# The head of a deformable-convolution stage: inputs asked for first, offsets beside norms, constants beside the sampling

## The chip, the cores and the metric

The kernel runs on one core of a Trainium2 chip. A core has TensorE (PE), VectorE (DVE), ScalarE (ACT), GpSimd (POOL) and SyncE (SP), which run their own instruction streams in order and meet through semaphores, and 16 DMA engines that SP, ACT and POOL give work to. The metric is the device time of one execution in microseconds, as the median of several; lower is better.

## The reference

The model has two layers; only the first half of layer 0 is touched here. For an image `x` of 2 x 128 channels x 64 x 64 pixels:

```python
x = x + L0_conv(ln_c(x))       # layer 0: deformable convolutions, then a small mixture of experts
t = t + L0_ffn(ln_t(t))
x = x + L1_conv(ln_c(x))       # layer 1: a depthwise convolution, a state-space scan, a gated output
t = t + L1_ffn(ln_t(t))        #          then experts that pick their tokens
```

`L0_conv` has four branches of kernel sizes 1, 1, 3 and 7, so 1 + 1 + 9 + 49 = 60 taps. For every pixel and tap, an ordinary convolution of the same size gives an offset in y and x and a mask (180 channels in all); the normalised image is sampled bilinearly at the shifted place, multiplied by the mask, and the samples of all taps are multiplied by the branch's weights and summed:

```python
offset = conv2d(x, off_w, off_b, pad); mask = 2 * sigmoid(conv2d(x, mod_w, mod_b, pad))
sampled = bilinear_sample(x, base_y + off_y, base_x + off_x) * mask     # outside the image: zero
y = einsum('bckhw,ock->bohw', sampled, reg_w)                            # then group norm and relu
```

A fifth branch uses the mean of the image; a 1 x 1 convolution fuses the five.

## The kernel before

**Tiling.** A group is 8 image rows, 512 pixels, handled as four tiles of 128 pixels (`GT`); an image has 8 groups (`NG`), and the batch has two images, `b` = 0 and 1.

**The norm of one group** (`norm_group`, L254 to L287). The input `xc` (128 channels x 512 pixels) is loaded on SP, transposed on PE (L264), copied to `xn` by ACT (L266), and normalised per pixel (`token_norm_gen`, L80: statistics on DVE, square root on ACT, then DVE). Eight DMAs on SP (L280) write `xn` into `table[b]` in DRAM: 67 x 67 places of 4 x 128 values, where a place holds a pixel and its three neighbours, so that one row read is one bilinear sample. `xn` is also transposed back (L271), copied by ACT to `padc`, and written by ACT's queue to `xp[b]`, the padded image (L283); a sum over `padc` (L286) serves the mean. `zero_table` (L236) writes the zero borders first: four rows and four columns of `table[b]`, and the rims of `xp[b]`, on SP.

**The offsets of one group** (`offset_stream`, L297). Rows of `xp` are loaded as `stage` on SP (`rows`, L357); ACT copies them seven times, shifted, into `ring` (`to_ring`, L362); PE does 49 products for each of four pairs of rows (`products`, L369); DVE adds the bias, and after each second pair `corners` (L388) works out indices and weights for half of the group.

**The sampling of one group** (`sample`, L535) goes through the 60 taps: four indirect gathers on POOL (L547) into one of six `v` buffers, bilinear weighting on DVE, transposes and summing on PE, a copy to `st` on ACT, and, two taps later, the product with the tap's weights `regw` (L597). The weights come in six chunks of ten taps; `load_chunk` (L231) loads one into one of four places.

**What sets the order.** There is no scheduler in this part: each engine runs its instructions in the order in which the program issues them. Python generators cut the side work into steps: `together` and `mixed` (L157) step several norms in turn, and `sample` takes after each tap one step of `conv` (the offsets of the next groups) and two or three steps of `rest` (three for the first group). `rest` holds the norm of image 1, then `more` (a second PSUM place for the offsets), then `position_matrices` (L845), which prepares layer 1. `self.pending` holds functions that `sample` calls after a counted number of taps.

**The head.** The program's first DMAs are three constants in `Env` (L61 to L66) and those of layer 1's `L1Conv.__init__` (L885 to L910). Then `run` (L457) opens the pools, writes the zero borders of image 0, normalises its eight groups three at a time, loads weights on ACT's queue (`load_weights`, L218) and four chunks on SP, writes the zero borders of image 1, works out the offsets of group 0, and starts to sample.

Of the kernel before, what the change touches and what calls it, by code (L numbers as in the profile page):

```python
# [3 lines left out]

# [51 lines left out]
class Env:  # L56
    def __init__(self, tc, ctx, d):
        self.tc, self.nc, self.d = tc, tc.nc, d
        cp = ctx.enter_context(tc.tile_pool(name="const", bufs=1))
        nc = self.nc  # L60
        self.ident = cp.tile([P, P], F32, name="ident")  # L61
        nc.sync.dma_start(out=self.ident, in_=d["c_ident"])
        self.gm16 = cp.tile([P, P], F32, name="gm16")
        nc.sync.dma_start(out=self.gm16, in_=d["c_gm16"])
        self.gm8 = cp.tile([P, P], F32, name="gm8")
        nc.sync.dma_start(out=self.gm8, in_=d["c_gm8"])  # L66
        self.zero = cp.tile([P, 512], F32, name="zero")
        nc.vector.memset(self.zero, 0.0)

# [107 lines left out]
class L0Conv:  # L177
# [40 lines left out]
    def load_weights(self):  # L218
        nc, d = self.env.nc, self.env.d
        nc.scalar.dma_start(out=self.wcen, in_=d["wcen"])  # L220
        nc.scalar.dma_start(out=self.wring, in_=d["wring"])
        nc.scalar.dma_start(out=self.wout, in_=d["wout"])
        nc.scalar.dma_start(out=self.obias, in_=d["obias"].partition_broadcast(P))
        nc.scalar.dma_start(out=self.base, in_=d["c_base"])
        nc.scalar.dma_start(out=self.gn, in_=d["gn"])
        nc.scalar.dma_start(out=self.gnf, in_=d["gnf"])
        for c in range(3):
            self.load_chunk(c)
        self.load_chunk(5)

    def load_chunk(self, c):  # L231

# [3 lines left out]
    def zero_table(self, b):  # L236
        nc, z = self.env.nc, self.env.zero
        t = self.table[b]
        rows = t.rearrange("(y x) e -> y x e", x=TW)
        for y in (0, 1, TW - 2, TW - 1):  # L240
            nc.sync.dma_start(out=rows[y], in_=z[:TW, :512])
        for x in (0, 1, TW - 2, TW - 1):
            nc.sync.dma_start(out=rows[2 : TW - 2, x, :], in_=z[: TW - 4, :])
        for y in (0, 3 + H):
            nc.sync.dma_start(
                out=self.xp[b][:, y : y + 3, :], in_=z[:, : 3 * (W + 6)].rearrange("p (y x) -> p y x", y=3)
            )

    def norm(self, b, pp, tag):
        for g in range(NG):  # L250
            yield from self.norm_group(b, g, self.sp, pp, tag)
        yield from self.norm_end(b)

    def norm_group(self, b, g, sp, pp, tag):  # L254


        env, nc = self.env, self.env.nc
        tab = self.table[b].rearrange("(y x) e -> y x e", x=TW)
        xp = self.xp[b]
        xc = sp.tile([P, 512], F32, name="xc")  # L260
        nc.sync.dma_start(out=xc, in_=env.d["x"][b, :, g * 512 : (g + 1) * 512])
        yield
        pt = pp.tile([P, GT, P], F32, name="nrm_pt", tag=tag)
        transpose4(nc, env.ident, pt, [xc[:, j * P : (j + 1) * P] for j in range(GT)])  # L264
        xn = sp.tile([P, GT, C], F32, name="xn")
        nc.scalar.copy(xn, pt)  # L266
        yield
        yield
        yield from token_norm_gen(env, sp, "n0", xn, xn, 1e-6)
        pb = pp.tile([P, GT, P], F32, name="pad_pt", tag=tag)  # L270
        transpose4(nc, env.ident, pb, [xn[:, j, :] for j in range(GT)])  # L271
        at = self.padc[g % 2][:, :, 3 : 3 + W]
        nc.scalar.copy(at, pb.rearrange("p j (y x) -> p (j y) x", x=W))
        for dy in range(2):
            for dx in range(2):
                q = 2 * dy + dx
                to = tab[2 - dy : 2 - dy + H, 2 - dx : 2 - dx + W, q * C : (q + 1) * C]
                to = to.rearrange("(t two) x c -> two x t c", two=2)
                for yl in range(2):
                    nc.sync.dma_start(  # L280
                        out=to[yl][:, g * GT : (g + 1) * GT, :], in_=xn[yl * W : (yl + 1) * W, :, :]
                    )
# [11 lines left out]
        self.normed.add(b)  # L294
        yield

    def offset_stream(self, runs):  # L297

        nc = self.env.nc
        chain = iter(())
        todo = deque()

        def piece():

            nonlocal chain
            if todo:
                wait, what = todo[0]
                if wait:  # L310
# [1 line left out]
                else:  # L312
# [1 line left out]
                    k, po, raw, end = what  # L314
                    nc.vector.tensor_tensor(raw[:, k % OT, :], po, self.obias, ALU.add)
                    if end:
                        yield from chain
                        chain = end()
            next(chain, None)
            yield  # L320

        for b, g, dst in runs:
            assert b in self.normed
            idx, w4 = dst or self.new_group(self.op)
            yb = 8 * g
            stage = self.rows(b, yb, 8)
            yield from piece()
            self.to_ring(stage, 0, 8)
            yield from piece()
            for k in range(GT):  # L330
                mats = self.products(2 * k)
                for i in range(7):
                    for m in mats[7 * i : 7 * i + 7]:
                        m()  # L334
# [14 lines left out]
                todo.append((5 if len(self.p_f) > 1 else 0, (k, self.po, raw, end)))  # L349
                if len(self.p_f) == 1:  # L350
                    yield from piece()
        while todo:
            yield from piece()
        for _ in chain:
            yield

    def rows(self, b, y0, n):  # L357
# [99 lines left out]
    def run(self, build, after):  # L457
# [3 lines left out]
        with ExitStack() as ctx:  # L461
# [24 lines left out]
            psum = ctx.enter_context(ExitStack())  # L486
            self.p_f = deque([pools(psum)("l0po", 1, space=PSUM)])
            early = psum.enter_context(ExitStack())
            p_m = pools(early)("l0pm", 1, space=PSUM)

            def more():

                early.close()
                self.p_f.append(pools(psum)("l0po2", 1, space=PSUM))
# [40 lines left out]
    def sample(self, b, g, idx, w4, conv, rest, pace):  # L535

        env, nc = self.env, self.env.nc
        pw = None
        for br, (k, _) in enumerate(BRANCH):
            for t in range(FIRST[br], FIRST[br] + k * k):  # L540
                tw = t % HT
                if tw == 0:
                    pw = self.p_w.tile([P, GT, HT, 4], F32, name="pw")
                    nc.vector.tensor_copy(pw, w4[:, :, t : t + HT, :])
                v = self.vp.tile([P, GT, 4 * C], F32, name="v")
                for j in range(GT):
                    nc.gpsimd.indirect_dma_start(  # L547
                        out=v[:, j, :],
                        out_offset=None,
                        in_=self.table[b],  # L550
                        in_offset=bass.IndirectOffsetOnAxis(ap=idx[:, j, t : t + 1], axis=0),
                    )
                v4 = v.rearrange("p j (q c) -> p j q c", q=4)


# [313 lines left out]
class L1Conv:  # L869
# [4 lines left out]
    def __init__(self, env, dp, wp, x2, x3):  # L874
        nc, d = env.nc, env.d
        self.env, self.dp, self.x2, self.x3 = env, dp, x2, x3
        self.pos = dp.tile([512 // CG, KP, NPOS, CG], F32, name="pos")

        def load(name, shape, src=None):
# [4 lines left out]
        self.wp = wp  # L884
# [19 lines left out]
        self.w1 = [wp.tile([P, 2, 4], F32, name=f"w1_{b}") for b in range(B)]  # L904
        for b in range(B):
            for h in range(2):
                nc.sync.dma_start(out=self.xsd[b][h * P : (h + 1) * P, 0:3], in_=env.zero[:, 0:3])
            for s in range(2):
                nc.sync.dma_start(out=self.att[b][s : s + 1, 0:3], in_=env.zero[0:1, 0:3])
                nc.sync.dma_start(out=self.att[b][s : s + 1, N + 3 :], in_=env.zero[0:1, 0:3])  # L910

    def convs(self, b, sp, pp):

# [694 lines left out]
def metaformer_kernel(ctx: ExitStack, tc: tile.TileContext, d: dict, out: bass.AP):  # L1608
# [7 lines left out]
    with tc.manual_schedule(engines={ET.PE, ET.DVE, ET.Activation, ET.Pool, ET.SP}), ExitStack() as l0:  # L1616
# [102 lines left out]
```

## Time and profile before

| | us |
|---|---|
| median of 3 runs | 8280.49 (8272.83 to 8282.75) |
| the profiled execution | 8332.4 |
| its span | 8330.6 |
| first table write of image 0 issued on SP | 45.19 |
| last table write of image 0 begun | 120.6 |
| first product of the offsets on PE | 164.35 |
| first gather on POOL | 197.88 |
| first gather of group 0's second half | 224.77 |

| engine | busy us | share | instructions |
|---|---|---|---|
| PE | 5808.5 | 70% | 27808 |
| DVE | 5729.7 | 69% | 8508 |
| ACT | 2120.9 | 25% | 4432 |
| POOL | 4590.5 | 55% | 4576 |

The span runs from the first to the last instruction of the profiled execution. In a line of the timeline, the first number is the start in us from the start of the span, the second is the duration in us, then come the engine (SPq and ACTq are DMA issues on those engines' queues), the line of the program, the operation, the tiles written and read, and how many instructions are merged; in brackets stands how long the engine had been idle and what ended that. In a line of the waits: who waited for whom, us in total, times, the longest.

### The profile page before, as it was taken

How to read it: one execution, taken by the hardware profiler on the slowest of the kernel's cores; microseconds unless marked ns; L12 is line 12 of the kernel's file. 1: busy time of each engine (PE TensorE's matmuls, PEld its weight loads, DVE VectorE, ACT ScalarE, POOL GpSimd, SP SyncE). 2: the span in 40 equal slices, each digit the busy share in tenths (PEclk: the TensorE clock that was granted, in tenths of full speed). 3: DMA queues.
4: the chain of work that ended last, by engine and by line, in shares of the span. 5: the costliest groups of instructions: out<-in, count | busy, mean ns of one | idle time of the engine just before them, and what ended most of it. 6: DMA issues, size and time to landing. Idle time of an engine off the chain costs nothing. (4 is left out here: it accounts for less than half of the span.)

```text
span 8330.6 us, 83751 instructions
## 1 busy us (share of the span) xinstructions
PE 5808.5 (70%) x27808; PEld 4000.1 (48%) x27808; DVE 5729.7 (69%) x8508; ACT 2120.9 (25%) x4432; POOL 4590.5 (55%) x4576
## 2 busy tenths in 40 slices
PE   2688888888888867766766676666755565855558
PEld 2456656666666644443434443344434444733335
DVE  1577777777777776777786667666647745669981
ACT  1111111111111113211111221112163344655540
POOL 0456666666666666666666666666534433347640
PEclk7788999999999988888888888788876665656568
DMA  4677666666666668867677777777653344434434
GB/s 128 185 249 216 195 207 203 205 213 197 207 203 206 208 212 261 270 213 234 218 240 203 228 204 223 219 206 216 176 166 135 127 110 107 128 106 149 145 124 141
DMA packets 636007, 1579.35 MB, mean 190 GB/s; under 512 B 167700, under 2 KB 247356, under 8 KB 623036
## 3 DMA queue, kind: packets, MB, share of 16 engines
q0 software_dynamic: 307200, 1006.88, 40.6%
q1 hardware_dynamic: 298284, 515.10, 19.5%
q10 hardware_dynamic: 30096, 52.03, 1.7%
q8 instruction: 226, 3.70, 0.2%
q14 instruction: 201, 1.65, 0.1%
HBM read 1456.11 MB, written 120.01 MB: 189 GB/s over the span
## 5 line engine op out<-in xcount | busy, mean ns | idle before, releaser
L547 POOL DMA_INDIRECT v<-table,idx x3840 | 3643.7, 949 | 2384.2 <-issue 1000.0
L597 PE MATMUL out<-st,regw 128*128 128x512 f32 x3840 | 2115.3, 676 | 161.2 <-issue 108.7
L558 DVE TENSOR_TENSOR v<-v,pw 128x1024 f32<-128x1024 f32 x960 | 1169.5, 1218 | 1060.9 <-DMA v<-table,idx 871.0
L568 PE MATMUL pst<-ident,v 128*128 128x128 f32 x7680 | 1240.2, 304 | 823.3 <-issue 529.5
L577 ACT COPY st<-pst 128x512 f32<-128x512 f32 x960 | 558.3, 585 | 4347.3 <-remote 2367.5
L568 PEld LDWEIGHTS pst<-ident,v 128*128 128x128 f32 x7680 | 1001.1, 157 | 1162.1 <-issue 786.9
L564 DVE TENSOR_TENSOR v<-v,low 128x512 f32<-128x512 f32 x1920 | 1318.0, 686 | 65.4
L563 DVE TENSOR_TENSOR low<-v,pw 128x512 f32<-128x512 f32 x1920 | 1329.0, 692 | 33.4
L1246 POOL TENSOR_TENSOR db<-du,bcb 128x512 f32<-128x512 f32 x512 | 660.0, 1293 | 937.2 <-DVE da L1303 897.4
L597 PEld LDWEIGHTS out<-st,regw 128*128 128x128 f32 x3840 | 762.0, 221 | 776.6 <-issue 713.7
L334 PEld LDWEIGHTS po<-wout,ring 128*128 128x128 f32 x5120 | 740.1, 198 | 366.5 <-issue 365.1
L334 PE MATMUL po<-wout,ring 128*128 128x147 f32 x5120 | 785.6, 299 | 167.4 <-issue 162.3
L1303 DVE TENSOR_TENSOR_SCAN da<-da,state,db 128x512 f32<-128x512 f32 x512 | 657.1, 1283 | 278.3 <-ACT da L1253 260.8
L1271 PE MATMUL py<-ident,sc 128*128 128x128 f32 x2048 | 463.0, 379 | 336.2 <-DVE sc L1313 335.1
L1271 PEld LDWEIGHTS py<-ident,sc 128*128 128x128 f32 x2048 | 338.6, 196 | 476.8 <-DVE sc L1313 441.5
L1313 DVE TENSOR_TENSOR sc<-da,bcb 128x512 f32<-128x512 f32 x512 | 354.2, 692 | 48.6 <-DVE da L1303 1.9
L1253 ACT ACTIVATE da<-delta,w_A_log 128x512 f32<-128x512 f32 x512 | 354.0, 692 | 17.3 <-DVE delta L1209 1.5
L972 PE MATMUL ps<-tm,X 120*88 120x48 f32 x2048 | 246.1, 299 | 62.9 <-ACT Y L924 22.5
L972 PEld LDWEIGHTS ps<-tm,X 120*88 120x88 f32 x2048 | 241.7, 213 | 94.4 <-issue 41.4
L959 PE MATMUL ps<-ident,hs 64*120 64x64 f32 x1408 | 142.1, 271 | 124.9 <-ACT X L924 69.8
L988 PE MATMUL ps<-ident,Y 88*64 88x88 f32 x768 | 108.1, 291 | 155.9 <-ACT img L924 100.1
L959 PEld LDWEIGHTS ps<-ident,hs 64*120 64x120 f32 x1408 | 125.5, 177 | 184.2 <-ACT X L924 89.5
(270 smaller groups left out, 4811.1 us busy)
## 6 DMA issues: line engine op xcount, KB each, us to landing
bcb<-bc SPq DMA_DIRECT2D x256, 512.0 KB
regw<-in_regw SPq DMA_DIRECT2D x66, 1280.0 KB
v<-table,idx POOLq DMA_INDIRECT x3840
yd<-ys ACTq DMA_DIRECT2D x128, 256.0 KB
yc<-yd SPq DMA_DIRECT2D x32, 1024.0 KB
gb<-gd SPq DMA_DIRECT2D x16, 2048.0 KB
wt<-in_weight SPq DMA_DIRECT2D x32, 1024.0 KB
tm<-pos SPq DMA_DIRECT2D x16, 1440.0 KB
```

The costliest lines, as they stand in the source:

```text
L334: m()
L547: nc.gpsimd.indirect_dma_start(out=v[:, j, :], out_offset=None, in_=self.table[b], in_offset=bass.IndirectOffsetOnAxis(ap=idx[:, j, t : t ...
L558: nc.vector.tensor_tensor(up, up, w, ALU.mult)
L563: nc.vector.tensor_tensor(low, v4[:, two, 2:4, :], w, ALU.mult)
L564: nc.vector.tensor_tensor(up[:, two], up[:, two], low, ALU.add)
L568: nc.tensor.matmul(pt[:, j, :], v4[:, j, q, :], env.ident, is_transpose=True, start=j == 0 and q == 0, stop=j == GT - 1 and q == 1,)
L577: nc.scalar.copy(st, pt.rearrange("p j t -> p (j t)"))
L597: nc.tensor.matmul(self.out[half], self.regw[t // CH][:, t % CH, half * P : (half + 1) * P], st, start=first, stop=last,)
L972: nc.tensor.matmul(ps[:, c, :], X[:, c0 + c, :], tm[:, :, c0 + c], start=True, stop=True)
L1246: nc.gpsimd.tensor_tensor(dbs[u], pieces[k]["du"][:, half, :], bcb[u // 2][:, 0, :], ALU.mult)
L1271: nc.tensor.matmul(out[:, j, :], what[:, j * P : (j + 1) * P], env.ident, is_transpose=True, start=first and j == 0, stop=last and j == GT ...
L1303: nc.vector.tensor_tensor_scan(s, s, dbs.pop(u), state[:, half, n : n + 1], ALU.mult, ALU.add)
```

## The change

There are five edits.

1. Constants. Two of the three in `Env` go to ACT's queue. Those of layer 1 move from `L1Conv.__init__` into a generator, `constants`, which `run` puts into the side stream ahead of `position_matrices`.
2. Input. All eight `xc` of image 0 are loaded at once, into two of the `v` buffers, which the sampling doesn't use yet; `load_weights` follows on ACT's queue, and it loads no chunks any more.
3. Norms and offsets. Two norms of image 0 are done, then the 14 rows that group 0 needs are loaded as one `stage0`. The other six go on three at a time: 24 steps first, then one piece of the offsets for every three steps. `offset_stream` takes the loaded rows as `ahead`. When the norms are through, chunk 0 is loaded and the offsets are finished.
4. Side stream. The zero borders of image 1 become steps of `norm`; chunks 1, 2 and 5 go into `pending`, after 1, 10 and 30 taps.
5. Gathers. For the first five taps of group 0, the gathers of the first half of the pixels are issued ahead, and those of the second half at each tap.

```diff
 class Env:
-        nc.sync.dma_start(out=self.gm16, in_=d["c_gm16"])
+        nc.scalar.dma_start(out=self.gm16, in_=d["c_gm16"])
...
-        nc.sync.dma_start(out=self.gm8, in_=d["c_gm8"])
+        nc.scalar.dma_start(out=self.gm8, in_=d["c_gm8"])
...
     def load_weights(self):
...
-        for c in range(3):
-            self.load_chunk(c)
-        self.load_chunk(5)
...
     def zero_table(self, b):
...
         for y in (0, 1, TW - 2, TW - 1):
             nc.sync.dma_start(out=rows[y], in_=z[:TW, :512])
+            yield
         for x in (0, 1, TW - 2, TW - 1):
             nc.sync.dma_start(out=rows[2 : TW - 2, x, :], in_=z[: TW - 4, :])
+            yield
...
     def norm(self, b, pp, tag):
+        yield from self.zero_table(b)
         for g in range(NG):
             yield from self.norm_group(b, g, self.sp, pp, tag)
...
-    def norm_group(self, b, g, sp, pp, tag):
+    def norm_group(self, b, g, sp, pp, tag, xc=None):
...
-        xc = sp.tile([P, 512], F32, name="xc")
-        nc.sync.dma_start(out=xc, in_=env.d["x"][b, :, g * 512 : (g + 1) * 512])
-        yield
+        if xc is None:
+            xc = sp.tile([P, 512], F32, name="xc")
+            nc.sync.dma_start(out=xc, in_=env.d["x"][b, :, g * 512 : (g + 1) * 512])
+            yield
...
-    def offset_stream(self, runs):
+    def offset_stream(self, runs, ahead=None):
...
-            stage = self.rows(b, yb, 8)
+            stage = ahead or self.rows(b, yb, 8)
...
-                        stage = self.rows(b, yb + 2 * k + 8, 2)
+                        stage = ahead[:, 2 * k + 8 :] if ahead else self.rows(b, yb + 2 * k + 8, 2)
...
     def run(self, build, after):
...
-            self.zero_table(0)
+            psum = ctx.enter_context(ExitStack())
+            right = lambda name: pools(psum)(name, 1, space=PSUM, side="right")
+            self.p_f = deque([right("l0po")])
+            cur = self.new_group(self.ip)
...
-                together([self.norm_group(0, g, sp, pp, "nrm") for g in range(NG)], 3)
-            self.load_weights()
-            self.zero_table(1)
-            for _ in self.norm_end(0):
-                pass
+                xs = []
+                for g in range(NG):
+                    if g % GT == 0:
+                        x = self.vp.tile([P, GT, 4 * C], F32, name="v")
+                    xs.append(x[:, g % GT, :])
+                    nc.sync.dma_start(out=xs[g], in_=env.d["x"][0, :, g * 512 : (g + 1) * 512])
+                self.load_weights()
+                for _ in self.zero_table(0):
+                    pass
+                norms = [self.norm_group(0, g, sp, pp, "nrm", x) for g, x in enumerate(xs)]
+                together(norms[:2], 2)
+
+                stage = sp.tile([P, 14, W + 6], F32, name="stage0", bufs=1)
+                nc.sync.dma_start(out=stage, in_=self.xp[0][:, 0:14, :])
+                others = Side()
+                others.add(mixed(norms[2:], 3))
+                for _ in range(24):
+                    others.step()
+                offsets = self.offset_stream([(0, 0, cur)], stage)
+                while others.todo:
+                    next(offsets)
+                    for _ in range(3):
+                        others.step()
+                self.load_chunk(0)
+                for _ in self.norm_end(0):
+                    pass
+                for _ in offsets:
+                    pass
...
+            self.pending = [(n, functools.partial(self.load_chunk, c)) for n, c in ((1, 1), (10, 2), (30, 5))]
...
-            cur = self.new_group(self.ip)
-            for _ in self.offset_stream([(0, 0, cur)]):
-                pass
...
     def sample(self, b, g, idx, w4, conv, rest, pace):
...
+        def gather(v, t, tiles):
+            for j in tiles:
+                nc.gpsimd.indirect_dma_start(
+                    out=v[:, j, :],
+                    out_offset=None,
+                    in_=self.table[b],
+                    in_offset=bass.IndirectOffsetOnAxis(ap=idx[:, j, t : t + 1], axis=0),
+                )
...
+                if b == 0 and g == 0 and t == 0:
+                    for i in range(5):
+                        vs[i] = self.vp.tile([P, GT, 4 * C], F32, name="v")
+                        gather(vs[i], i, range(0, 2))
+                if t in vs:
+                    v = vs.pop(t)
+                    gather(v, t, range(2, GT))
+                else:
+                    v = self.vp.tile([P, GT, 4 * C], F32, name="v")
+                    gather(v, t, range(GT))
...
 class L1Conv:
...
+    def constants(self):
+        nc, d, wp = self.env.nc, self.env.d, self.wp
...
         self.saw = load("sa_conv_w", [14, 1])
+        yield
...
                 nc.sync.dma_start(out=self.att[b][s : s + 1, N + 3 :], in_=self.env.zero[0:1, 0:3])
+            yield
...
-        conv.run(position_matrices(env, mixer.pos), after)
+        conv.run(chain(mixer.constants(), position_matrices(env, mixer.pos)), after)
```

More of the change, by code (lines that the diff above doesn't have):

```diff
@@ L3 @@
 from contextlib import ExitStack
+from itertools import chain
 import concourse.bass as bass
@@ L295, in norm_end @@
         yield
-    def offset_stream(self, runs):
+    def offset_stream(self, runs, ahead=None):
         nc = self.env.nc
-        chain = iter(())
+        arith = iter(())
         todo = deque()
         def piece():
-            nonlocal chain
+            nonlocal arith
             if todo:
@@ L316, in piece @@
                     if end:
-                        yield from chain
-                        chain = end()
-            next(chain, None)
+                        yield from arith
+                        arith = end()
+            next(arith, None)
             yield
         for b, g, dst in runs:
-            assert b in self.normed
+            assert ahead or b in self.normed
             idx, w4 = dst or self.new_group(self.op)
             yb = 8 * g
-            stage = self.rows(b, yb, 8)
+            stage = ahead or self.rows(b, yb, 8)
             yield from piece()
@@ L351, in offset_stream @@
                     yield from piece()
+            ahead = None
         while todo:
             yield from piece()
-        for _ in chain:
+        for _ in arith:
             yield
@@ L485, in run @@
             self.p_o = pool("l0py", 2, space=PSUM)
-            psum = ctx.enter_context(ExitStack())
-            self.p_f = deque([pools(psum)("l0po", 1, space=PSUM)])
+            self.pending = [(n, functools.partial(self.load_chunk, c)) for n, c in ((1, 1), (10, 2), (30, 5))]
             early = psum.enter_context(ExitStack())
-            p_m = pools(early)("l0pm", 1, space=PSUM)
+            p_m = pools(early)("l0pm", 1, space=PSUM, side="right")
             def more():
                 early.close()
-                self.p_f.append(pools(psum)("l0po2", 1, space=PSUM))
+                self.p_f.append(right("l0po2"))
                 yield
-            cur = self.new_group(self.ip)
-            for _ in self.offset_stream([(0, 0, cur)]):
-                pass
             conv, rest = Side(), Side()
@@ L537, in sample @@
         env, nc = self.env, self.env.nc
-        pw = None
+        pw, vs = None, {}
+        def gather(v, t, tiles):
[6 more added lines that the diff above has]
+                )
         for br, (k, _) in enumerate(BRANCH):
@@ L544, in sample @@
                     nc.vector.tensor_copy(pw, w4[:, :, t : t + HT, :])
[L545 to L552, printed above, removed]
+                if b == 0 and g == 0 and t == 0:
[8 more added lines that the diff above has]
+                    gather(v, t, range(GT))
                 v4 = v.rearrange("p j (q c) -> p j q c", q=4)
@@ L877, in __init__ @@
         self.pos = dp.tile([512 // CG, KP, NPOS, CG], F32, name="pos")
+        self.wp = wp
+    def constants(self):
+        nc, d, wp = self.env.nc, self.env.d, self.wp
         def load(name, shape, src=None):
@@ L882, in load @@
             return t
-        self.wp = wp
         self.c1w = load("conv1d_w", [P, 2, 4])
@@ L906, in __init__ @@
             for h in range(2):
-                nc.sync.dma_start(out=self.xsd[b][h * P : (h + 1) * P, 0:3], in_=env.zero[:, 0:3])
+                nc.sync.dma_start(out=self.xsd[b][h * P : (h + 1) * P, 0:3], in_=self.env.zero[:, 0:3])
             for s in range(2):
-                nc.sync.dma_start(out=self.att[b][s : s + 1, 0:3], in_=env.zero[0:1, 0:3])
-                nc.sync.dma_start(out=self.att[b][s : s + 1, N + 3 :], in_=env.zero[0:1, 0:3])
+                nc.sync.dma_start(out=self.att[b][s : s + 1, 0:3], in_=self.env.zero[0:1, 0:3])
+                nc.sync.dma_start(out=self.att[b][s : s + 1, N + 3 :], in_=self.env.zero[0:1, 0:3])
+            yield
     def convs(self, b, sp, pp):
```

## The prediction

> **What bounds the kernel now.** I read the page's slices first: POOL, which gathers for the sampling, shows nothing before the second slice and then 4 to 6 tenths for three quarters of the span. Sampling is the long stage, and nothing of it runs in the first 200 us. The list of waits over the first 500 us says how long:
>
> ```profile
> POOL v L547 <- DMA stage<-xp: 197.4, 1, 197.4
> POOL v L547 <- DVE idx L431: 24.5, 1, 24.5
> ```
>
> So a head of 224.77 us (the gather that the second line ends with) stands before the first complete tap. SyncE's queue over that head, in order of time:
>
> ```profile
> 20.92 7.46 SPq L243 DMA_DIRECT2D table<-zero  x4
> 28.43 1.22 SPq L245 DMA_DIRECT2D xp<-zero  x2
> 29.70 5.99 SPq L261 DMA_DIRECT2D xc<-in_x  x3
> 45.19 17.88 SPq L280 DMA_DIRECT2D table<-xn  x24
> 63.17 1.50 SPq L261 DMA_DIRECT2D xc<-in_x  x3
> 73.22 18.16 SPq L280 DMA_DIRECT2D table<-xn  x24
> 91.48 1.03 SPq L261 DMA_DIRECT2D xc<-in_x  x2
> 101.68 19.51 SPq L280 DMA_DIRECT2D table<-xn  x16
> 121.24 5.17 SPq L234 DMA_DIRECT2D regw<-in_regw  x4
> 129.56 15.23 SPq L241 DMA_DIRECT2D table<-zero  x4
> 144.83 5.33 SPq L243 DMA_DIRECT2D table<-zero  x4
> 150.20 3.35 SPq L245 DMA_DIRECT2D xp<-zero  x2
> 153.60 41.78 SPq L359 DMA_DIRECT2D stage<-xp  x5
> ```
>
> One queue strings everything together: zeros of table 0, norms in threes whose input is asked for only behind the previous three's writes, weights, zeros of table 1, and only then the rows for the offsets. The timeline gives the rest of the head, the four products of 49 matmuls each, whose first one waits for the ring's copies and whose last one ends with the bias addition:
>
> ```profile
> 162.10 3.76 ACT L365 COPY ring<-stage 128x512 f32<-128x512 f32 x7 [58.03 <-DMA stage<-xp]
> ...
> 164.35 0.97 PE L334 MATMUL po<-wcen,ring 128*128 128x180 f32 x2 [60.91 <-ACT ring L365]
> ...
> 219.59 0.35 DVE L315 TENSOR_TENSOR raw<-po,obias 128x180 f32<-128x180 f32 x1 [12.62 <-PE po L334]
> ```
>
> Behind the head I looked at stretches, for the tile st alone; the fourth pair of figures is ACT's copies of it, one per tap (then clock, DMA share, GB/s):
>
> ```profile
> 332.00:384.00 52.00, 16.76 (x26) 6.31 (x25) 0.00 (x0) 3.51 (x6) 0.80 0.71 219
> ...
> 2000.00:2500.00 500.00, 183.97 (x340) 64.11 (x338) 0.00 (x0) 49.63 (x85) 0.91 0.68 204
> ```
>
> Six taps take 52 us while image 1 is normalised; later 85 take 500, 5.88 us each. No later stage waits for a fixed moment, so what the head loses the end loses.
>
> [...] from 15 to 25 us the DMA share is 0.07 at 25 to 26 GB/s, about one sixteenth. [...]
>
> **The change, part by part.**
>
> *Removed from the front.* 8.5 us of constants on SP (2.12 to 10.64); two gm loads go to ACT. All eight x loads go out at about 1.2 us, so the input no longer waits behind table writes.
>
> *The zeros become the first limit.* Table writes overlap the zeroed border, so they wait for it. [...] first table write near 43.5. The first two norms are ready by then: ACT was held 12.7 us after wout before (107.97 to 120.67); shared with x and zeros I allow it until 23, and the first norm took 5.6 us from copy to table write (39.58 to 45.19).
>
> *Norms 0 to 4.* 16 table writes at 17.88/24 = 0.745 us end at 55.4. With three xn buffers, norm 4's copy waits for norm 1's writes; landing is about 3 us (the last xc load issued near 92.0 to PE at 94.85): 58.4. From the last copy of a trio to its first write took 2.75 us (42.44 to 45.19): 61.2. 24 writes: 79.1; landed 82.1. The stage load of 14 rows sits between and is ready.
>
> *Where the offsets start.* Only 24 steps are taken ahead, exactly norms 2, 3, 4. But then the first round issues the ACT copies of norms 5, 6, 7 before the ring copies. The third needs norm 4's buffer, so at 82.1 it goes, at 82.7 the ring copies begin, and PE starts 2.25 later (162.10 to 164.35): 85.0. The offsets thus run beside the tail of three norms, not beside six.
>
> *From there to sampling.* Before: 164.35 to 224.77 = 60.4 us. Added on PE: 12 transposes of norms 5 to 7, 2.45 + 1.2 = 3.6 us. Their normalising takes DVE until about 8 us after the third copy; PE's first 28 matmuls last as long (28/49 of 13.5), so no further wait. The last 24 writes leave SP by about 107; the first half's gathers come near 122. Second half: 85.0 + 60.4 + 3.6 = 149. Against 224.77: **-76 us**.
>
> *Zeros of table 1, chunks.* They have no producer to wait for; SP runs ahead to them right after chunk 0, around 110, [...] ended by 145, hidden by products 1 to 3 and the corners. If that cover were gone, up to 26 us would come back at the first taps. Chunks 1, 2 and 5 are issued at taps 1, 10, 30 for products at 12, 22, 52; ten taps at 5.88 are 59 us: nothing. That SP no longer does this ahead of the offsets (121.24 to 153.60) is in the 76 already.
>
> *Half gathers of five taps.* Eight more gathers at 1.25 us go before the second half's indices. Tap 0 starts as before; for taps 1 to 4 POOL needs 2.5 us rather than 5.0, while DVE needs 4: at most 4 us, I take **-2**.
>
> *The first group's taps.* Norm 1 now starts 8 steps later, at three steps a tap, so its pieces fall otherwise. Before, the sum over padc stands in the tap of its own transposes, and DVE idles 6.65 us for it (at 325.47), and 2.4 us more at statistics and normalising; after, the sum falls a tap later, but the statistics come in the tap of their own transposes and wait for the same queue on PE, some 6.5 us. Net up to -2.5 us in each of 8 cycles of 26 us; as the trace doesn't show that order, bounds +20 and -20, I take **-8**. Also taps 2 to 3 stood 26 us apart (247.16 to 273.48), 15 more than in a later cycle, when table writes met gathers and two stores; three plain taps now go ahead. Bounds 0 and -15: **-5**.
>
> *Constants in the side stream.* 21 small DMAs on SP, hidden, as SP idles between norms. The exponential on ACT waits at worst for its load and has a 1.28 us table load and a reload: 0 to +5, I take **+2**. The gm loads on ACT: 0.9 us before the weights, hidden by the zeros; uncovered +1.
>
> Sum: -76 - 2 - 8 - 5 + 2 = -89 us. The profiled execution took 8332.4 with a span of 8330.6, so 8243 for it; the median of the three runs is 8280.5, 52 lower, and a stretch of the head should be equally long in both: **8191 us**, 1.1% less. A change under 0.2% (17 us) couldn't be told from none.
>
> **Rivals.** *Fuller overlap, 17%.* [...] PE starts at 72 and the first group gives its whole -39: 76 + 13 + 39 - 2 = 126, so about 8155. For it: DMA reached 448 GB/s (110 to 115 us) with large rows. [...]
>
> *The first group takes part back, 18%.* SP gets to table 1's zeros late [...]: +26, and the new order of norm 1 costs +20 instead of -8: -76 + 26 + 20 + 2 - 2 = -30 at the worst; half of both is about 8227. For it: SP's waits [...] (7.14 us for one row under load). Against: SP has 40 us in hand.
>
> *Slower, 2%.* The statistics' wait in the new order of norm 1 comes on top of the old wait for the sum and holds DVE, PE and gathers in turn. It decides where 76 + 17 us are lost, 11.6 us in each of eight cycles, from 26 to 38 us; with 13 us a cycle it is 8280.5 - 76 + 104 = 8308. Against: the longest idle now is 6.65, and one more of that size in each cycle gives 53 in all, 8257.
>
> *No change, 2%:* ACT can't free itself from weight issue (12.7 us became 70), and norms start late.
>
> **How the numbers follow.** Likeliest, 61%: -65 to -112, so 8168 to 8216. Eight in ten, with most of the two side cases: 8156 to 8230. Faster 0.95 (61 + 17 + most of 18, less a point), same 0.03, slower 0.02.
>
> **What would show it.** First table write near 43; PE's first product near 85, directly after ring copies that follow the last xn copy; the 11th gather (second half's indices) near 149; table 1's zeros on SP between 105 and 145; cycles of norm 1 near 24 us. Wrong if: PE starts products before 72 or after 100, the 3-tap cycle leaves 20 to 29 us, or later taps leave 5.88 us.

## The result, and the profile after

| | before | after |
|---|---|---|
| median (range), us | 8278.98 (8272.83 to 8282.75, 4 runs) | 8167.34 (8160.73 to 8177.89, 4 runs) |
| ratio, 95% interval | | 0.9867 [0.985, 0.9884] |
| profiled execution's span | 8330.6 | 8176.1 |
| first table write of image 0 | 45.19 | 48.98 |
| last table write of image 0 begun | 120.6 | 100.3 |
| first product of the offsets | 164.35 | 79.01 |
| first gather of group 0's second half | 224.77 | 145.26 |
| first store of image 1's indices (about 76 taps in, early in the second group) | 744.0 | 652.9 |

The kernel became 112 us faster (interval 96 to 124); 89 were forecast, just outside this interval. In the list of waits over the first 500 us, POOL's wait of 197.4 us for `stage` is gone. What stands ahead of the sampling now are two waits for indices, for the first half and then for the second:

```profile
POOL v L567 <- DVE idx L434: 132.4, 2, 113.1
```

SyncE's queue in order of time, as it was shown of the kernel before:

```profile
1.18 6.79 SPq L488 DMA_DIRECT2D v<-in_x  x8
9.66 16.73 SPq L239 DMA_DIRECT2D table<-zero  x4
26.44 7.49 SPq L242 DMA_DIRECT2D table<-zero  x4
33.98 6.96 SPq L245 DMA_DIRECT2D xp<-zero  x2
48.98 11.72 SPq L282 DMA_DIRECT2D table<-xn  x16
60.74 0.61 SPq L496 DMA_DIRECT2D stage<-xp  x1
61.46 40.42 SPq L282 DMA_DIRECT2D table<-xn  x48
101.92 0.60 SPq L232 DMA_DIRECT2D regw<-in_regw  x1
...
103.05 8.38 SPq L239 DMA_DIRECT2D table<-zero  x3
...
134.70 0.99 SPq L263 DMA_DIRECT2D xc<-in_x  x1
```

The two pauses for input between table writes are gone, and the zeros of table 1 come after the table writes, while PE works. What still stands in front is the zeros of table 0: 31 us of issuing (9.66 to 40.94), and 8 more until the first write. The timeline of ACT and PE shows what the offsets waited for:

```profile
23.89 0.33 ACTq L224 DMA_DIRECT2D obias<-in_obias  x1
34.91 0.33 ACTq L225 DMA_DIRECT2D base<-in_c_base  x1
41.16 0.34 ACTq L226 DMA_DIRECT2D gn<-in_gn  x1
...
42.09 1.28 ACT L268 ACT_TABLE_LOAD   x1 [42.09 <-DMA xp<-zero]
...
76.28 0.58 ACT L268 COPY xn<-nrm_pt 128x512 f32<-128x512 f32 x1 [5.15 <-DMA table<-xn]
76.77 3.76 ACT L368 COPY ring<-stage 128x512 f32<-128x512 f32 x7
...
81.70 0.59 ACT L268 COPY xn<-nrm_pt 128x512 f32<-128x512 f32 x1 [1.07 <-DMA table<-xn]
```

```profile
79.01 0.97 PE L336 MATMUL po<-wcen,ring 128*128 128x180 f32 x2 [7.97 <-ACT ring L368]
...
125.35 0.57 PE L336 MATMUL po<-wcen,ring 128*128 128x180 f32 x2 [3.61 <-issue]
```

ACT's small weight loads are strung out until 41.7 us, although each takes 0.33 us to issue, so ACT's first copy comes only when SP has issued its last zeros (40.94). The ring's copies follow the second of the last three norms' copies, not the third. And the fourth product starts 3.6 us after PE was ready for it.

The 79.5 us of the head divide at instants of these profiles (with those of the run with the offsets behind the norms, below): the end of SP's table-write issue moved from 121.2 to 98.9 with input asked for first (-22.3, of which the run with input asked for late, below, gives back 16); the products' start against that end from +43.1 to -7.9, as weights, chunks and the zeros of table 1 no longer stand between (-51.0); offsets begun beside norms -12.0; and from first product to second half 66.3 instead of 60.4 us (+5.8). The split is read from instants: no run puts weights, chunks and the zeros of table 1 back in front, so the -51.0 rests on what the two queues show. The sum closes by construction, as the third run's instants cancel in it; they lie within 3 us of the changed kernel's where both have the same work.

### The profile page after: what moved, and what is told of

It reads as the page before. It is cut to its first block, busy times and chain, and to the rows that moved or that the text cites. A ratio compares the mean times of both kernels' runs of the same rounds, so it can differ in the third digit from the quotient of the medians.

```text
span 8176.1 us, 83726 instructions
## 1 busy us (share of the span) xinstructions
PE 5782.7 (71%) x27808; PEld 4002.8 (49%) x27808; DVE 5727.6 (70%) x8508; ACT 2122.1 (26%) x4433; POOL 4589.2 (56%) x4576
## 5 line engine op out<-in xcount | busy, mean ns | idle before, releaser
L635 PE MATMUL out<-st,regw 128*128 128x512 f32 x3840 | 2073.0, 665 | 117.9 <-issue 86.5
L336 PE MATMUL po<-wout,ring 128*128 128x147 f32 x5120 | 806.0, 301 | 216.3 <-issue 212.4
```

Of the source, the lines that this page charges most:

```text
L635: nc.tensor.matmul(self.out[half], self.regw[t // CH][:, t % CH, half * P : (half + 1) * P], st, start=first, stop=last,)
```

## Experiments

The runs below come in three sets, each on another chip, and the core's speed in the sampling differs between them: the kernel before took 8343, 8294 and 7557 us, with clocks of 0.80 to 0.84, while the instants of the head stay the same within 3 us up to the start of the products. Only kernels of one set are compared in us; across sets, by their ratio to the kernel before. A set's intervals are some 0.2% either way (17 us), so small effects are read from instants in the profiles. Behind the start of the products, instants differ between sets too.

### Is the excess over the forecast real?

Both kernels were run once more, unedited (first set).

> The changed kernel once more, unedited, for a second profile and more times. The measured gain of 112 us is 23 more than the forecast sum. Theory A (the excess is real and lies in the sampling of image 0): the groups of image 0 are stored at 323 to 325 us intervals again, against 327.4 in the kernel before, and the median is 8155 to 8180. Theory B (the excess is the spread of single executions): the interval moves by 2 us or more between the two profiles of the same kernel.

> The kernel before, unedited, for a second profile of it. Theory A: intervals between the stores of image 0's groups of 327 to 328 us again, and the head to the first gather of the second half 224 to 226 us. Theory B: intervals between 324 and 327 us, and the whole span nearer to the median (8275 to 8285) than the first profile's 8330.6.

The changed kernel took 8233.78 us, the one before 8342.56; ratio 0.9871 [0.9852, 0.989], -109 us. In microseconds from the span's start:

| | before | before again | after | after again |
|---|---|---|---|---|
| second half's first gather | 224.8 | 227.3 | 145.3 | 150.6 |
| first tap of the second group begun | 652.0 | 654.5 | 558.0 | 561.3 |
| first store of image 1's indices | 744.0 | 748.5 | 652.9 | 654.7 |
| eighth store | 3035.8 | 3044.4 | 2923.5 | 2945.9 |
| mean interval of stores (the last is half as long) | 327.4 | 328.0 | 324.4 | 327.3 |
| last group of image 1 done (fuse weights asked for) | 6073.9 | 6073.6 | 5928.3 | 5987.8 |
| span | 8330.6 | 8336.9 | 8176.1 | 8249.9 |

The changed kernel's own interval moved by 2.9 us, which is theory B's outcome; the kernel before kept its interval (328.0), which is theory A's. What decides is the set. From the first store to the end, the four profiles of the first set take 7585 to 7595 us, whichever kernel it is; the four of the second set take 7532 to 7546, one of them the kernel before with wide zeros, and all four have a mean interval of 324.2 to 324.6. The first pair of profiles falls on both sides: 7587 before, 7523 after. The profiled execution before, 8332.4 us, also lies outside the runs beside which it stands (8272.83 to 8282.75) and inside those of the first set (8323.15 to 8351.73). So the 63 us by which the first pair of spans differs beyond the first store (-154.5 against -91.1) come, as far as the record tells, from two sets that were compared with each other, not from the change; the second pair, of one set, shows 7 us less at the end than at the first store (-87.0 against -93.8).

The head and the first group are worth -94 and -93 (at the second group's first tap), and no later gain appears within a set. The medians are 16 to 18 us further down, with -94 and -93 at the edge of their intervals (-96 and -92 us); whether some of that is real stays open.

### Zero rows in 128 pieces

```diff
         for y in (0, 1, TW - 2, TW - 1):
-            nc.sync.dma_start(out=rows[y], in_=z[:TW, :512])
+            flat = t[y * TW : (y + 1) * TW, :].rearrange("x e -> (x e)").rearrange("(p f) -> p f", p=P)
+            nc.sync.dma_start(out=flat, in_=z[:, : TW * 4 * C // P])
...
         for x in (0, 1, TW - 2, TW - 1):
-            nc.sync.dma_start(out=rows[2 : TW - 2, x, :], in_=z[: TW - 4, :])
+            nc.sync.dma_start(out=rows[1 : TW - 2, x, :], in_=z[: TW - 3, :])
```

In the changed kernel:

> The changed kernel with the zero borders written [...] rows as 128 pieces of 1072 bytes, columns of 64 pixels. Theory 1 (the zero rows [...] set the first table write and hold ACT's weight issues until 42 us): ACT is free by 18 to 25 us, the first table write comes at 25 to 32 us instead of 49, the first gather of the second half at 122 to 130 instead of 145.3, and the time falls by 15 to 22 us. Theory 2 (ACT is held by its own large weight load, and SP's zeros only fill that time): ACT is free at 38 to 42 us as now, and the time moves by less than 5 us.

The edit widens the columns too (63 places become 64), so rows and columns aren't told apart. 8215.8 us, ratio 0.9848 [0.9826, 0.9869], 18 us under the changed kernel of the same set. ACT and SP of this run:

```profile
20.97 0.34 ACTq L224 DMA_DIRECT2D obias<-in_obias  x1
...
25.45 1.28 ACT L269 ACT_TABLE_LOAD   x1 [25.45 <-DMA table<-zero]
```

```profile
9.52 7.88 SPq L240 DMA_DIRECT2D table<-zero  x4
21.01 2.44 SPq L243 DMA_DIRECT2D table<-zero  x4
...
32.35 11.96 SPq L283 DMA_DIRECT2D table<-xn  x16
```

ACT comes free 16.6 us earlier, the first table write 16.6, the first product 16.5 (62.46). Theory 1 holds: nothing was changed on ACT's queue, so SP's transfers held ACT's weight loads, and the zeros set the start of everything. The second half's first gather, 133.5, is 3.5 us later than expected, for the late addition seen below.

The same edit in the kernel before (second set):

> The kernel before with the zero borders written [...] nothing else changed. Theory 1 (each set of zeros costs the kernel before [...] some 23 us, of which 14 to 16 are uncovered): the first norms' input arrives at 20 to 25 us instead of 38, the first product begins 26 to 34 us earlier than 164 to 167, and the time falls by 25 to 33 us. Theory 2 (SP's issue of so many transfers is what costs): less than 10 us.

The 23 us of theory 1 was an estimate; 4 x 134 KB of rows at the 25 to 26 GB/s that the kernel before shows from 15 to 25 us make some 21. The run took 8257.15 us, ratio 0.9957 [0.9941, 0.9973]: -37 us by the medians of the set, -22 to -49 by the interval. Its timeline:

```profile
20.71 2.79 PE L104 MATMUL nrm_pt<-ident,xc 128*128 128x128 f32 x12 [20.71 <-DMA xc<-in_x]
```

Input arrives at 20.7 instead of 38.4, the first product begins at 132.8 instead of 164.4, the second half at 192.9 instead of 224.8. So 32 of the old head's 225 us were two sets of zero borders in their narrow form. The change covered the second set, and kept the first.

### Offsets after the norms

```diff
-                while others.todo:
-                    next(offsets)
-                    for _ in range(3):
-                        others.step()
+                others.drain()
```

> The changed kernel with all eight norms finished before the first piece of the offsets; everything else stays. Theory 1 (the offsets only run beside the tail of the last norms, most of the gain is the freed SP queue): PE starts the products at 92 to 97 us instead of 79, the second half's first gather comes at 154 to 160 us, and 9 to 14 us are lost. Theory 2 (running beside the norms hides the products): 40 to 55 us are lost.

8255.27 us, ratio 0.9899 [0.988, 0.9919], 21 us over the changed kernel of the set, with spans only 4 apart (8254.1 and 8249.9). In its timeline:

```profile
91.03 0.97 PE L336 MATMUL po<-wcen,ring 128*128 128x180 f32 x2 [3.93 <-ACT ring L368]
```

12 us later than in the changed kernel (78.9); the second half comes at 159.3, 9 to 14 later. Products that start so soon leave no room for theory 2. "Beside six norms" is worth some 12 us of the head, not the 54 of the products; the loss in time is 4 to 21, and not known more closely.

### Input asked for late

Each input is loaded, into the same `v` buffers, at its norm's first step (third set):

```diff
-                    nc.sync.dma_start(out=xs[g], in_=env.d["x"][0, :, g * 512 : (g + 1) * 512])
...
+        else:
+            nc.sync.dma_start(out=xc, in_=env.d["x"][b, :, g * 512 : (g + 1) * 512])
```

> The changed kernel with each group's input asked for at that norm's first step, as in the kernel before (into the same buffers), instead of all at the start; the order of all else stays. Theory 1 (the input standing behind table writes on SP was a large part of the old head): the first table write comes within 4 us of 49, but norms 2 to 4 start their writes 8 to 12 us later than 61, norms 5 to 7 again so, PE starts the products at 96 to 106 us instead of 79, and 18 to 28 us are lost. Theory 2 (table writes, which take 0.75 us each whatever is done, set the pace anyway): less than 8 us are lost.

7468.11 us against 7556.59 of the kernel before; ratio 0.9885 [0.9862, 0.9908]. SP's queue has the pauses again:

```profile
45.21 11.69 SPq L284 DMA_DIRECT2D table<-xn  x16
56.94 0.61 SPq L497 DMA_DIRECT2D stage<-xp  x1
57.59 1.39 SPq L266 DMA_DIRECT2D v<-in_x  x3
68.50 1.92 SPq L284 DMA_DIRECT2D table<-xn  x3
```

Norms 2 to 4 write 7 us later, norms 5 to 7 at 97.9, the products start at 94.7, 16 later, and so does the second half: 156.4, against 140.2 in the run of the changed kernel (without the early gathers, below) whose last bias additions are as regular as this one's. Theory 1's direction is right, its size a little high at the products. By ratio to the kernel before (0.9867 to 0.9871 for the changed kernel) the loss in time is inside the intervals; but the next run, of the same set, is 16.5 us faster, and the ranges don't overlap (7466.33 to 7476.77, 7441.92 to 7459.59). If the place of the constants is worth nothing in time, the late input thus costs there about what it costs at the products.

### Constants in front

The generator `constants` is run through at the end of `L1Conv.__init__`, and leaves the side stream.

```diff
         self.wp = wp
+        for _ in self.constants():
+            pass
...
-        conv.run(chain(mixer.constants(), position_matrices(env, mixer.pos)), after)
+        conv.run(position_matrices(env, mixer.pos), after)
```

> The changed kernel with layer 1's constants loaded at the start again, before the input. Theory 1 (SP's queue is the path from its first instruction on): the input and the zeros go out 8.5 us later, the first table write comes at 56 to 58 us, the second half's first gather 7 to 9 us later, and 6 to 9 us are lost. Theory 2 (ACT's weight issues, held to 42 us, cover it): the first table write moves by less than 3 us and nothing measurable is lost.

7451.65 us, ratio 0.9856 [0.9832, 0.988]. The first table write came at 50.97 and the first product at 80.9, each 2 us later than in the changed kernel; the second half's first gather came at 143.7, 3.5 later than the 140.2 just named. Theory 2's outcome, for a reason that it only half names: in this order ACT issues its large load ahead of SP's traffic and is free at 28.5 us, and the zeros alone set the first write. Removing 8.5 us from the head of SP's queue gained some 2 us there, and nothing that the times show.

### The gathers ahead

```diff
-                    for i in range(5):
+                    for i in range(0):
                         vs[i] = self.vp.tile([P, GT, 4 * C], F32, name="v")
```

> The changed kernel without the gathers ahead: each tap's four gathers are issued at the tap. In the changed kernel the bias addition of the third product came 3 to 6 us late (13.45 us after the second's would be regular; PE's fourth product began 16.6 to 19.5 us after the third), during the ten early gathers. Theory 1 (the gathers, by their DMA or by POOL, hold up DVE): the fourth product begins 13.4 to 13.6 us after the third, the second half's first gather comes 3 to 6 us earlier than in the changed kernel, and the first taps then follow each other at 5 rather than 4 us; in time -2 to +4 us. Theory 2 (the 1280 KB of weights and the zero rows fill the DMA at that moment, whatever the gathers do): the gap stays at 16 us or more, and 2 to 6 us are lost.

8196.8 us (second set), ratio 0.9874 [0.9852, 0.9896]. VectorE's bias additions, of the changed kernel and then of this run:

```profile
108.33 0.34 DVE L317 TENSOR_TENSOR raw<-po,obias 128x180 f32<-128x180 f32 x1 [13.11 <-PE po L336]
124.95 0.34 DVE L317 TENSOR_TENSOR raw<-po,obias 128x180 f32<-128x180 f32 x1 [11.20 <-remote]
```

```profile
108.07 0.34 DVE L317 TENSOR_TENSOR raw<-po,obias 128x180 f32<-128x180 f32 x1 [13.11 <-PE po L336]
121.53 0.35 DVE L317 TENSOR_TENSOR raw<-po,obias 128x180 f32<-128x180 f32 x1 [8.04 <-PE po L336]
```

Without the early gathers the addition follows the last at 13.46 us, with them at 16.62 (19.53 in the second profile, 19.55 with the offsets behind the norms). These are runs of the first two sets. In the third set the ten gathers delay nothing: with constants in front, where they are issued from 116.9 to 128.3 us, the addition is on time, 13.46 us after the last (111.65):

```profile
125.11 0.34 DVE L317 TENSOR_TENSOR raw<-po,obias 128x180 f32<-128x180 f32 x1 [8.04 <-PE po L336]
```

So the delay was seen only beside the early gathers, but they alone don't make it. Without the gathers ahead, the second half comes at 140.2, 5 to 10 us earlier; then tap 1 starts 5.26 us after tap 0 instead of 3.91. The first store is at 650.1 against 652.9 and 654.7. Theory 1 holds in this set: the gathers ahead take back what they give.

### Norm of image 1 at the first step

```diff
     def norm(self, b, pp, tag):
-        yield from self.zero_table(b)
...
                 self.load_chunk(0)
+                for _ in self.zero_table(1):
+                    pass
```

> The changed kernel with the zero borders of image 1 all issued before the sampling (at the same place of SP's queue), so that they take no steps and the norm of image 1 begins at the first step, as in the kernel before. Theory 1 (the order of the norm's pieces against the taps costs): the cycle of three taps is 26 to 26.3 us instead of 24.7 to 24.9, and from the second half's first gather to the first group's store of image 1's indices it takes 515 to 522 us instead of 504 to 508; 8 to 15 us are lost. Theory 2 (the first group went faster for the gathers ahead or for later chunks): both stay as in the changed kernel.

8196.73 us (second set), ratio 0.9873 [0.9851, 0.9895]. Table writes of image 1, this run's and then the changed kernel's:

```profile
196.42 5.47 SPq L281 DMA_DIRECT2D table<-xn  x8
...
353.30 5.45 SPq L281 DMA_DIRECT2D table<-xn  x8
```

```profile
218.70 6.70 SPq L282 DMA_DIRECT2D table<-xn  x8
...
368.38 7.36 SPq L282 DMA_DIRECT2D table<-xn  x8
```

These are the second and the eighth in both runs: a cycle of 26.15 us, as before the change (26.06 and 26.26), against 24.95 (24.68 in the second profile). From the second half's first gather to the first store it takes 514.1 us, against 507.6 and 504.1, and 519 to 521 before. The order costs what theory 1 says for the cycle; of the 14 us that this stretch gained it accounts for about half. The rest shows in the first taps (in this run tap 3 starts 32.6 us after tap 0, before the change 43.8), but its cause wasn't tried apart. In time the 8 to 15 us of theory 1 don't show: the ratio is 0.9873, the changed kernel's 0.9867 and 0.9871.

### A faster version

With wide zeros, the third thing in the way was the start of the ring's copies. Twelve steps of the other norms ahead, and two for each piece:

```diff
-                for _ in range(24):
+                for _ in range(12):
                     others.step()
...
-                    for _ in range(3):
+                    for _ in range(2):
```

> The changed kernel with wide zeros, and with the offsets begun after 12 instead of 24 steps of the other norms and two instead of three steps for each piece, so that the ring copies stand ahead of norms 5 to 7. Theory 1 (the start of the products is set by the ACT copies issued ahead of the ring's): PE starts the products at 47 to 52 us instead of 62.5, the second half's first gather comes at 112 to 120 instead of 133.5, and the time is 14 to 22 us below wide zeros alone (33 to 40 below the changed kernel). Theory 2 (interleaved norms then hold PE, as their transposes wait for table writes): the products start early but take 75 us or more, and less than 5 us is won over wide zeros.

8156.94 us, ratio 0.9832 [0.9807, 0.9857], 40 us under the changed kernel's two variants of that set. On ACT the ring's copies now stand ahead of all of norms 5 to 7:

```profile
45.78 0.59 ACT L269 COPY xn<-nrm_pt 128x512 f32<-128x512 f32 x1 [4.74 <-DMA table<-xn]
...
49.41 3.76 ACT L369 COPY ring<-stage 128x512 f32<-128x512 f32 x7 [0.40 <-ACT padc L276]
...
62.44 0.59 ACT L269 COPY xn<-nrm_pt 128x512 f32<-128x512 f32 x1 [3.37 <-PE nrm_pt L105]
```

PE starts at 51.7, the second half at 117.3, inside what theory 1 expects. Again, and without the gathers ahead, in the third set:

> The version with wide zeros and earlier offsets again, for its interval: 0.981 to 0.985 of the kernel before, 30 to 38 us under the changed kernel.

> The version with wide zeros and earlier offsets, without the gathers ahead. Theory 1 (early gathers hold up the last products as much as they help the first taps): the second half's first gather comes 1 to 3 us earlier (PE's small gaps near 106 us go), and the time is within 4 us of the version with them. Theory 2 (the gathers ahead pay once nothing else is late): 3 to 6 us are lost.

7413.25 us, ratio 0.9809 [0.979, 0.9828], and 7428.28, 0.9831 [0.9808, 0.9854]; second halves at 116.1 and 115.5, first stores at 566.6 and 568.5. The version beats both kernels; by its two ratios it is 0.35 to 0.6% below the changed one, and in the third set 38 us below the changed kernel with its constants in front. Without the gathers nothing is lost at the first store beyond 2 us; the 15 us between the medians, with ranges that overlap, are not explained by anything in the profiles.

## Why the prediction was right

**The mechanism** was: the head on SP's queue is shortened, and the end moves with it. It held. Forecast for the head -76, measured -79.5 and -76.7 in the two pairs; for the first group -13 net, measured from tap 0 to the second group's first tap 406.9 instead of 422.2 us in the mean, -15.3. The total of -89 was -94 and -93 at the second group's first tap.

**Zeros as the first limit**: right, and the wide zeros showed it. The term was a little small: first write at 48.98 instead of 43.5. The 43.5 was my estimate: how the bytes divide over the DMA engines, on which it rested, is shown by no trace here. Its side step, "I allow it until 23" for ACT, was wrong: ACT was free at 42.1, and the first write came 6.9 us later, as in the run with wide zeros (25.45 and 32.35). So the zeros set the first write by way of ACT, which they held up; I had reckoned only with slower transfers under shared load, which was an estimate too.

**Where the offsets start**: 79.0 instead of 85.0, with the wrong reason written down. The step "the first round issues the ACT copies of norms 5, 6, 7 before the ring copies" took three norms to enter together. `mixed` takes in one at each step, so they run staggered, and only norms 5 and 6 stand ahead. The same stagger lets norm 2 write without its trio: norms 2 to 4 began to write at 61.46, where 61.2 was forecast, although the first write came 5.5 us late. So one slip, the stagger, took back the late first write and 6 us more, and the next term gave 2 to 8 us away again; the fine forecast of 149 against 145 to 151 owes something to luck.

**From first product to sampling**: 66.3 and 71.7 instead of 64.0. I put the early gathers at no cost to the head; in these two profiles an addition came 3 to 6 us late beside them. With that, "half gathers", given as -2, was worth about 0.

**Zeros of table 1 hidden**: right. The 26 us that I gave them was an estimate on the same footing; before, issuing them took 24 us (129.56 to 153.55). They were issued from 103 to 135 us, and the first taps waited for none of it: 4.80 us from the second half's first gather to tap 0, 4.89 before.

**The order of norm 1**, -8, measured -9 to -13 over eight cycles (26.06 and 26.26 before, 24.95 and 24.68 after); undone, 6 to 10 us came back between the second half and the first store. **Taps 2 to 3**, -5: the pause didn't go; it was 26.3 us and is 24.4, one tap later, so about -2. **Constants**, +2: inside what can't be told; but the removal from the front was worth some 2 us of the head, not 8.5.

**The rivals.** "Fuller overlap" asked for PE's start by 72; it was 79. "The first group takes part back" did not happen. "Slower" was refuted by cycles of 25 us. Of "no change", the reason came in part: ACT was held to 42 us, where that rival asked for 70. The median, 8167, lies 1 us below the likeliest case's 8168, as the medians of this change came out 16 to 18 below what head and first group show.

## What to carry to other kernels

Read a head as one chain of queue entries: ask for each what it waits for, and move whatever nobody waits for behind what somebody does; here, by the instants, weights, chunks and the second set of zeros were worth 51 us, and starting products beside norms 12. Look at the DMA share during "cheap" fills: 0.07, at 25 to 28 GB/s, is hardly more than the part of one engine in sixteen (0.0625), and a reshaped fill brought the first product forward by 17 us in one kernel and by 32 in the other. When generators are interleaved, write out the real order of issue on each engine before saying what runs beside what. And before a difference of 1% is looked for in a late stage of two profiles, see whether one chip made both.

## What the runs showed of the hardware

- **Zero fills in SP's queue held up issues on ACT's queue.** Four small loads behind ACT's large one were issued at 23.9, 34.9, 41.2 and 41.7 us with narrow zeros, at 21.0, 21.5, 24.3 and 25.0 with wide ones. With narrow zeros but ACT's large load issued ahead of SP's input and zeros (constants in front), it was 21.1, 24.4, 27.6 and 28.2, so the order matters too. While narrow zero rows are moved, the DMA share is 0.07 at 25 to 28 GB/s (15 to 25 us before the change, 20 to 25 us after it). Over how many engines the rows go, narrow or wide, isn't shown, nor by what means the other queue's issues wait.
- **PE stood still with nothing in the profile to show for it, in the runs on one chip and not in those on another.** The faster version is the same kernel in the second and the third set. Ten products in the pause behind its fourth tap were spread from 143.4 to 153.1 us in the second set, single matmuls 2 us apart, and took 1.4 us in the third:

```profile
146.10 0.28 PE L337 MATMUL po<-wout,ring 128*128 128x147 f32 x1 [1.80 <-issue]
148.20 0.41 PE L337 MATMUL po<-wout,ring 128*128 128x147 f32 x1 [1.81 <-issue]
```

```profile
141.53 1.42 PE L337 MATMUL po<-wout,ring 128*128 128x147 f32 x10
```

  From 500 to 2500 us, PE's waits of this kind before products come to 190.8 us in the first of these profiles, and to 124 to 202 us in all ten of the first pair and the first two sets (146.5 before the change and 192.1 after it, in the first pair); in the four of the third set none is listed. DVE's late addition goes the same way: 2 to 6 us in the profiles with early gathers of the former, none in the three of the third set.

```profile
PE po L337 <- issue: 190.8, 241, 4.3
```

  What PE and DVE wait for there isn't shown.
- **The sampling took 16% longer in one set than in another, and the head hardly differed.** The faster version took 324.2 us from store to store in the second set and 278.7 in the third, with the second half's first gather at 117.3 and 116.1 us. The granted clock was 0.802 and 0.837, 4% apart. Whether the waits above are part of the rest isn't shown, nor whether it is the chip or the hour, as each set ran on one chip only.
